# First stage of a four-layer graph network: roots by square root and reciprocal, work moved between GpSimd, VectorE and ScalarE

## The chip, the core and the metric

The kernel runs on one core of one Trainium2 chip. The core has a matrix engine (PE, with its weight loads shown apart as PEld), a vector engine (DVE), a scalar engine (ACT), GpSimd (POOL) and SyncE (SP), which here issues nearly all DMA transfers. The engines run side by side, each works its own instructions strictly in order, and they wait for each other by semaphores. SBUF is the working memory; PSUM takes the products of PE and can be read by DVE and ACT.

The metric is the device time of one execution in microseconds, the median of several runs.

## What is computed

The input is x, 128 graphs of 128 nodes with 128 features, and adj, an integer matrix of 128 x 128 for each graph, which the input generator fills with 0 and 1. Four layers of the form x = x + L(relu(layernorm(x))) follow each other. Cut to what matters here:

```python
def _layernorm(x, axis=-1, eps=1e-5):
    return (x - mean(x)) / sqrt(var(x) + eps)

# layer 0: relations r = 1..7
mask = (adj == r);  degree = clip(mask.sum(axis=2), 1e-6)
agg += ((mask / degree) @ h) @ rel_weights[r]
out = relu(layernorm(agg + h @ self_w.T + self_b) * gamma + beta)

# layer 1
D = abs(h[:, :, None, :] - h[:, None, :, :])     # every pair of nodes, 128 features
p = D @ W1.T + b1                                 # 64 features for every pair
p = leaky(normalised over all graphs and pairs) @ W2.T
A = softmax(where(adj > 0, p, -9e15));  y = A @ h ...

# layers 2 and 3: attention with adj > 0 as the mask
```

The dear part is D and its product: 128 graphs times 128 x 128 pairs. Since |a - b| is symmetric the kernel computes half of the pairs.

## The kernel before, in words

**Stages.** The first stage (to about 1528 us) does layer 0 and, tile by tile, the pair products of layer 1, which it stores to HBM (HP) together with their statistics. The second (to about 2330 us) reads them back, normalises and scores them and ends layer 1. The third does layers 2 and 3. The change touches the first stage alone.

**Tiles of pairs.** Graphs ("batches" in the code) are numbered b = 0 to 127, four of them (G) form a group, and there are 32 groups. Each batch has NT = 4 tiles of pair differences, tile i = 4 b + t. For one tile the steps are:

- ("d", i), `difference`, L311: one instruction of 128 x 2048 elements. If t is in ON_POOL = {1, 3} it is GpSimd's, else VectorE's. GpSimd reads both operands from SBUF (XE); VectorE reads one from SBUF and the other, x itself, from PSUM (XP). Tile t = 0 (BY_MAX) takes a maximum, the others a difference. The result goes to a tile d with two buffers for each of the two engines (tags d0, d1).
- ("abs", i), L352: ScalarE takes the absolute value in place, for t = 1 to 3.
- ("hp", i), L321 and L324: PE's products into PSUM, with two buffers.
- ("hs", i), L335: ScalarE copies the product to SBUF; ("st", i), L342 and L343: VectorE takes its statistics.

So 8 of the 16 tiles of a group are GpSimd's and 8 are VectorE's.

**The chain of a group.** `chain(g)` computes layer 0 for the four batches of a group and the input of the pair loop, some groups ahead of it. Its steps: load x and adj; `mask`, adj == 1 (GpSimd, L439), and its row sums (VectorE); `mv`, mean and variance of x (VectorE, L429 and L431); `rs`, the inverse root; `hn`, the normalised x with relu (ScalarE, four instructions, L452); transposes (PE) and their copies (ScalarE, L465); the products with the weights; `o`, the sum (VectorE); `mvo`, `rso`, `oc` and `on`, the second norm with gamma and beta from PSUM; `end`, the new x; `mvx` and `rsx` with the statistics for layer 1, and `h1`, its normalised relu (ScalarE, L493), from which the tiles start. In between GpSimd writes `m8` (L517), the mask adj > 0 as bytes, for the later stages.

A root, three in each chain, is four small GpSimd instructions on 128 x 4 elements: `rsqrt` adds eps (L224) and raises to the power of -0.5 (L225); `shift` multiplies with the mean (L280) and changes the sign (L281), which gives the bias of the following norm.

**What sets the order.** The steps are not run as they are written. Each `step(name, engine, cost, after, rank, work)` names its engine, an assumed cost in us, what it waits for and a rank; `_ordered` plays all steps of the stage through with these costs and a hop of 0.4 us between engines, always taking the step that can start first, and issues the instructions in the order so found. An engine then keeps that order whatever the real durations are. A difference waits, by its step, for the earlier difference i - 2 and for the product of tile i - 4, the earlier user of its buffer.

**The first microseconds.** The chains of the groups 0 and 1 run before a branch that asks whether adj holds anything above 1 (the path for that is not taken here), while all of adj is read for that question; the pair loop begins behind it at 48 us and runs freely from about 77 us.

The functions that the diff touches:

Of the kernel before, what the change touches and what calls it, by code (L numbers as in the profile page):

```python
# [14 lines left out]
OP = mybir.AluOpType  # L15
# [14 lines left out]
ROW = P + 2 * KH  # L30
ON_POOL = {1, 3}
BY_MAX = 0
AHEAD = 2
# [135 lines left out]
def tile_gnn_stack(ctx: ExitStack, tc: tile.TileContext, a: dict, out: bass.AP):  # L169
# [20 lines left out]
    mhalf = const.tile([P, 1], F32, name="mhalf")  # L190
    nc.gpsimd.memset(mhalf, -0.5)
    ones = const.tile([P, P], F32, name="ones")
    nc.vector.memset(ones, 1.0)
# [67 lines left out]
    with tc.tile_pool(name="c0", bufs=1) as c0, tc.tile_pool(name="p0", bufs=2) as p0, ExitStack() as ctx0:  # L261
# [14 lines left out]

        def shift(mv, rs):

            nb = small.tile([P, G], F32, name="lnnb")
            nc.gpsimd.tensor_tensor(nb, mv[:, :, 0], rs, OP.mult)  # L280
            nc.gpsimd.tensor_scalar(nb, nb, -1.0, None, op0=OP.mult)  # L281
            return nb


# [10 lines left out]
        def step(name, engine, cost, after, rank, work, takes=(), gives=()):  # L295
            steps.append((name, engine, cost, after, takes, gives, rank, work))

        XE, XW, diffs, linear, halves, stats = {}, {}, {}, {}, {}, {}

        def difference(i):  # L300

            b, t = divmod(i, NT)
            xe, k = XE[b // 2], b % 2
            on_pool = t in ON_POOL
            d = p0.tile([P, 2, KC, P], F32, tag=f"d{int(on_pool)}", name="d")
            x = xe[:, k, 0:P] if on_pool else XP[b // 2 % 2][:, k, :]
            ahead = xe[:, k, 1 + KC * t:]
            ahead = bass.AP(tensor=ahead.tensor, offset=ahead.offset,
                            ap=[list(ahead.ap[0]), [KH, 2], [1, KC], [1, P]])
            eng = nc.gpsimd if on_pool else nc.vector  # L310
            eng.tensor_tensor(d, ahead, x[:, None, None, :].to_broadcast([P, 2, KC, P]),  # L311
                              OP.max if t == BY_MAX else OP.subtract)
            diffs[i] = d.rearrange("p h k i -> p h (k i)")
# [40 lines left out]
        def pairs(i):  # L354

            b, t = divmod(i, NT)
            n, by_max = b // 2, t == BY_MAX
            engine, cost, rank = ("Pool", 4.22, i - 3) if t in ON_POOL else ("DVE", 2.2, i - 2)
            step(("d", i), engine, cost, [("again", n), ("d", i - 2), ("hp", i - 4)], rank, lambda: difference(i))
            if not by_max:  # L360
# [40 lines left out]
        def chain(g, agg=None, again=None):  # L401
# [22 lines left out]
            def moments(name):  # L424
# [5 lines left out]
                for k in range(G):  # L430
                    nc.vector.bn_aggr(mv[:, k, :], st[:, k, :])  # L431

            def roots(last=False):
                rs = t["rs"] = RS1[:, g] if last else small.tile([P, G], F32, name="lnrs")
                rsqrt(rs, t["mv"][:, :, 1])
                t["nb"] = shift(t["mv"], rs)

# [10 lines left out]
            def centred(dst, src, func=AF.Identity):  # L448
                if dst not in t:
                    tile0(dst)  # L450
                for k in range(G):
                    nc.scalar.activation(t[dst][:, k, :], t[src][:, k, :], func, bias=t["nb"][:, k:k + 1],  # L452
                                         scale=t["rs"][:, k:k + 1])

            def shared():
# [44 lines left out]
            else:  # L500
# [3 lines left out]
            step(("deg", g), "DVE", 0.6, own("mask"), s0 + 3.1, degree)  # L504
            step(("rs", g), "Pool", 1.95, own("mv"), s0 + 5, roots)
            step(("most", g), "Pool", 0.25, own("deg"), s0 + 5.1, at_least)
            step(("per", g), "DVE", 0.15, own("most"), s0 + 7, lambda: nc.vector.reciprocal(t["deg"], t["deg"]))
            step(("hn", g), "ACT", 1.55, own("rs"), s0 + 7, lambda: centred("hn", "x", AF.Relu))
            step(("share", g), "Pool", 1.05, own("per"), s0 + 9, shared)
            step(("pt", g), "PE", 0.55, own("hn"), s0 + 9, lambda: turned("hn"), takes=("sm",))  # L510
            step(("hT", g), "ACT", 0.5, own("pt"), s0 + 9.5, lambda: copied("hT", "pt"), gives=("sm",))
            step(("pm", g), "PE", 0.55, own("share", "hT"), s0 + 11, lambda: turned("mask"), takes=("sm",))
            step(("maskT", g), "ACT", 0.5, own("pm"), s0 + 12, lambda: copied("maskT", "pt"), gives=("sm",))
            step(("ph", g), "PE", 1.05, own("hT") + ["small"], s0 + 11.1, projected, takes=("sm",))
            step(("hw", g), "ACT", 0.5, own("ph"), s0 + 13, lambda: copied("hw", "ph"), gives=("sm",))
            step(("m8", g), "Pool", 1.5, own("load"), s0 + 11,
                 lambda: nc.gpsimd.tensor_scalar(M8[g], t["adj"], 0, None, op0=OP.is_gt))  # L517
            step(("po", g), "PE", 2.05, own("maskT", "hw"), s0 + 14, gathered, takes=("sm",))
            step(("o", g), "DVE", 0.6, own("po", "agg") + ["selfb"], s0 + 15, joined, gives=("sm",))
            step(("mvo", g), "DVE", 1.05, own("o"), s0 + 15.1, lambda: moments("o"))  # L520
            step(("rso", g), "Pool", 1.95, own("mvo", "hn"), s0 + 17, roots)
            step(("oc", g), "ACT", 1.55, own("rso"), s0 + 18, lambda: centred("o", "o"))
# [3 lines left out]
            step(("mvx", g), "DVE", 1.05, own("end"), s0 + 21.1, lambda: moments("MV1"))  # L526
            step(("rsx", g), "Pool", 1.95, own("mvx", "oc", "m8"), s0 + 23, lambda: roots(True))
            for half in range(2):
# [1073 lines left out]
```

## Time and profile before

| | |
|---|---|
| runs | 2803.65 us median of 3 (2803.29 to 2803.67) |
| profiled execution, span | 2798.6 us |
| around the span in that comparison | 5.05 us (median less span) |
| PE / DVE / ACT / POOL busy over the span | 2453.5 / 2474.2 / 2391.9 / 1720.2 us |
| first stage, steady part, one group | 45.6 us |
| first stage's pair loop ends | about 1528 us |

The page's busy times are means over stages with different limits; POOL's 61%, for instance, is near 95% in the first stage and small in the second. So the steady part of the first stage is read by itself below, group by group of sixteen tiles. In the rows, "x256" is the number of instructions, then come total busy us and mean ns of one, then the idle time of the engine just before them and what ended most of it.

### The profile page before, as it was taken

Reading aid. Unit: us, or ns where it says so; the run is one execution under the profiler, and the core shown is the slowest. Engines: PE = TensorE matmul, PEld = TensorE weight load, DVE = VectorE, ACT = ScalarE, POOL = GpSimd, SP = SyncE. Lnnn points to the kernel's source line nnn. Section 1 sums busy time; section 2 is a strip of 40 time slices with the busy share of each in tenths; the row PEclk is TensorE's granted clock in tenths of the full one; section 3 lists DMA queues with packets and bytes.
Section 4 is the critical chain, followed back from the end, with each engine's and each line's share of the span. In section 5 each row is a group of like instructions: output and inputs, shape, how many; then the busy total and the mean of one; then the engine's idle time right before and its main releaser. Section 6 shows DMA issues by size and latency. Waiting matters only on the chain.

```text
span 2798.6 us, 41745 instructions
## 1 busy us (share of the span) xinstructions
PE 2453.5 (88%) x14521; PEld 1178.8 (42%) x14521; DVE 2474.2 (88%) x4712; ACT 2391.9 (85%) x2837; POOL 1720.2 (61%) x1629
## 2 busy tenths in 40 slices
PE   3899999999999999999997798888888886999986
PEld 2333333333333333333332244444444444777775
DVE  4899999999999999999998588888888886899876
ACT  4799999999999999999997778877878765888975
POOL 6699999999999999999986001111000115555642
PEclk8899999999999999999999899999999998999998
DMA  7454555554555555554545999999999971121110
GB/s 285 169 207 202 204 207 212 213 211 200 207 202 208 207 218 207 207 211 200 207 203 217 418 410 412 411 413 411 411 412 413 413 266 46 46 67 59 58 31 25
DMA packets 179802, 652.40 MB, mean 233 GB/s; under 512 B 30963, under 2 KB 98678, under 8 KB 130422
## 3 DMA queue, kind: packets, MB, share of 16 engines
q1 hardware_dynamic: 179136, 649.39, 58.6%
q8 instruction: 120, 1.97, 0.3%
q14 instruction: 108, 0.88, 0.1%
q10 hardware_dynamic: 438, 0.17, 0.0%
HBM read 337.22 MB, written 312.28 MB: 232 GB/s over the span
## 4 chain that ended last, share of the span: by engine, by line
ACT 35%; PE 22%; DVE 21%; DMA 8%; issue 7%; POOL 5%; SPq 0%; ACTq 0%; DVEq 0%; POOLq 0%
ACT d L352 14%; ACT hs L335 10%; PE hp L321 5%; PE ps L853 5%; DVE z L896 4%; DVE d L311 3%; DMA rows<-sk 3%; POOL d L311 3%; DMA z<-hp 2%; DMA u<-rows 2%; PE hp L324 2%; PE pk L860 2%; ACT h L1206 2%; PE pv L1322 2%; ACT h L493 1%
## 5 line engine op out<-in xcount | busy, mean ns | idle before, releaser
L311 POOL TENSOR_TENSOR d<-xe 128x2048 f32<-128x2048 f32 x256 | 1074.1, 4201 | 59.0 <-PE hp L321 53.8
L321 PE MATMUL hp<-d,w1T 128*64 128x512 f32 x4096 | 997.1, 602 | 123.5 <-ACT hs L335 83.9
L352 ACT ACTIVATE d<-d 128x2048 f32<-128x2048 f32 x384 | 734.4, 1935 | 41.8 <-DVE d L311 22.9
L311 DVE TENSOR_TENSOR d<-xe,xp 128x2048 f32<-128x2048 f32 x256 | 579.4, 2263 | 4.7 <-PE hp L321 2.7
L321 PEld LDWEIGHTS hp<-d,w1T 128*64 128x64 f32 x4096 | 285.4, 137 | 642.1 <-issue 480.6
L335 ACT COPY hs<-hp 128x1024 f32<-128x1024 f32 x512 | 516.7, 1028 | 30.7 <-PE hp L324 24.0
L942 POOL TENSOR_TENSOR x<-x,bt 128x512 f32<-128x512 f32 x32 | 43.8, 1367 | 684.8 <-DMA x<-x 641.3
L342 DVE BATCH_NORM_STATS2 st<-hs 128x6 f32<-128x512 f32 x512 | 349.1, 682 | 43.5 <-ACT hs L335 43.1
L343 DVE BATCH_NORM_STATS2 st<-hs 128x6 f32<-128x512 f32 (+1 forms) x512 | 329.0, 643 | 0.0
L896 DVE SCALAR_TENSOR_TENSOR z<-z 128x2048 f32<-128x2048 f32 x128 | 295.1, 2306 | 21.7 <-ACT z L878 21.7
L878 ACT ACTIVATE z<-z,bias,scale 128x2048 f32<-128x2048 f32 x128 | 267.3, 2088 | 19.0 <-DMA z<-hp 19.0
L882 ACT ACTIVATE zr<-z,bias,scale 128x2048 f32<-128x2048 f32 x128 | 267.4, 2089 | 4.7 <-DMA z<-hp 3.8
L324 PE MATMUL hp<-both_t,xw 128*64 128x512 f32 x1024 | 268.1, 595 | 0.0
L853 PE MATMUL ps<-z,w2z 128*32 128x512 f32 x1024 | 143.8, 634 | 81.6 <-DVE z L896 81.6
L860 PEld LDWEIGHTS pk<-pick,su 128*128 128x128 f32 x1024 | 126.1, 194 | 134.4 <-DVE su L874 88.2
L860 PE MATMUL pk<-pick,su 128*128 128x16 f32 x1024 | 138.5, 267 | 17.6 <-DVE su L874 17.6
L1322 PE MATMUL pv<-wr,e 128*128 128x128 f32 x1024 | 140.5, 283 | 5.9 <-DVE e L1299 4.0
L853 PE MATMUL ps<-z,w2l 128*32 128x512 f32 x1024 | 143.1, 628 | 0.0
L324 PEld LDWEIGHTS hp<-both_t,xw 128*64 128x64 f32 x1024 | 80.7, 138 | 141.2 <-issue 141.2
L853 PE MATMUL ps<-zr,w2r 128*32 128x512 f32 x1024 | 139.9, 619 | 0.0
L1322 PEld LDWEIGHTS pv<-wr,e 128*128 128x128 f32 x1024 | 128.1, 196 | 13.3 <-DVE e L1299 4.1
L1299 DVE SCALAR_TENSOR_TENSOR e<-e,ps 128x512 f32<-128x512 f32 x160 | 106.9, 677 | 26.1 <-ACT ps L1296 25.4
(243 smaller groups left out, 3828.1 us busy)
## 6 DMA issues: line engine op xcount, KB each, us to landing
hp<-hs SPq DMA_DIRECT2D x128, 2048.0 KB, 6.3
z<-hp SPq DMA_DIRECT2D x256, 1024.0 KB, 14.3
x<-x SPq DMA_DIRECT2D x118, 256.0 KB, 11.6
u<-rows SPq DMA_DIRECT2D x32, 384.0 KB, 11.4
x<-in_x_dram SPq DMA_DIRECT2D x32, 256.0 KB, 3.0
adj<-in_adj_dram SPq DMA_DIRECT2D x32, 256.0 KB, 3.3
part<-in_adj_dram SPq DMA_DIRECT2D x16, 512.0 KB, 7.8
out_dram<-x SPq DMA_DIRECT2D x32, 256.0 KB, 2.4
```

The lines of the kernel that those rows point to most:

```text
L311: eng.tensor_tensor(d, ahead, x[:, None, None, :].to_broadcast([P, 2, KC, P]), OP.max if t == BY_MAX else OP.subtract)
L321: nc.tensor.matmul(hp[64 * hh:64 * hh + 64, c:c + 512], w1T2 if by_max else w1T, d[:, hh, c:c + 512], start=True, stop=not by_max, skip_gr ...
L324: nc.tensor.matmul(hp[64 * hh:64 * hh + 64, c:c + 512], XW[i // NT // 2][:, i // NT % 2, :], both_t.rearrange("p h k i -> p h (k i)")[:, h ...
L335: nc.scalar.copy(halves[b][:, t, :], linear.pop(i))
L342: nc.vector.bn_stats(st[:, 2 * t, :], hs[:, 0:512])
L343: nc.vector.bn_stats(st[:, 2 * t + 1, :], hs[:, 512:1024 - P * last])
L352: nc.scalar.activation(diffs[i], diffs[i], AF.Abs)
L853: nc.tensor.matmul(ps[32 * c:32 * c + 32, :], w[:, w0:w0 + 32], v[:, 512 * c:512 * c + 512], start=j0 == 0, stop=w is w2r, skip_group_chec ...
L860: nc.tensor.matmul(pk[:, kk, 0:16], su[:, kk, :], pick.rearrange("p h j -> p (h j)"), start=True, stop=True)
L882: nc.scalar.activation(zr, z1, AF.Relu, bias=bias1, scale=scale1[:, 0:1])
L896: nc.vector.scalar_tensor_tensor(z0, z0, 0.01, z0, op0=OP.mult, op1=OP.max)
L1322: nc.tensor.matmul(t[pv][:, k % 2, hd, :], t[e][:, hd, :], flat[:, at:at + P], start=True, stop=True)
```

## The change

- A root is now a ScalarE square root of variance + eps (step `sd`, `sdo`, `sdx`), followed on VectorE by a reciprocal and one scalar_tensor_tensor that makes the bias, minus mean times root. eps is a new constant tile. GpSimd has no part in it any more.
- `hn`, the first of the three norms, moves from ScalarE to GpSimd (four tensor_scalar, multiply and add with a value per row); its relu moves into ScalarE's copy of the transpose, which is there already.
- Nine of the sixteen tiles of a group are GpSimd's: beside t = 1 and 3 also tile 2 of the group's fourth batch. The waits for the earlier difference and the earlier user of the buffer are looked up for the engine concerned.
- `m8` is made by a minimum with 1 and a maximum with 0 in place of a comparison.
- The assumed costs of these steps are changed accordingly, so the order of the whole stage is found anew.

```diff
+EXTRA_ON_POOL = (3, 2)
...
+    eps = const.tile([P, 1], F32, name="eps")
+    nc.gpsimd.memset(eps, EPS)
...
-        def shift(mv, rs):
-            nb = small.tile([P, G], F32, name="lnnb")
-            nc.gpsimd.tensor_tensor(nb, mv[:, :, 0], rs, OP.mult)
-            nc.gpsimd.tensor_scalar(nb, nb, -1.0, None, op0=OP.mult)
-            return nb
...
+        def by_pool(i):
+            b, t = divmod(i, NT)
+            return t in ON_POOL or (b % G, t) == EXTRA_ON_POOL
+
+        def earlier(i, n):
+            return [j for j in range(i) if by_pool(j) == by_pool(i)][-n] if i >= 3 * n else -1
...
-            engine, cost, rank = ("Pool", 4.22, i - 3) if t in ON_POOL else ("DVE", 2.2, i - 2)
-            step(("d", i), engine, cost, [("again", n), ("d", i - 2), ("hp", i - 4)], rank, lambda: difference(i))
+            engine, cost, rank = ("Pool", 4.22, i - 3) if by_pool(i) else ("DVE", 2.2, i - 2)
+            step(("d", i), engine, cost, [("again", n), ("d", earlier(i, 1)), ("hp", earlier(i, 2))], rank,
+                 lambda: difference(i))
...
+            def deviation():
+                t["sd"] = small.tile([P, G], F32, name="lnsd")
+                nc.scalar.activation(t["sd"], t["mv"][:, :, 1], AF.Sqrt, bias=eps)
+
             def roots(last=False):
                 rs = t["rs"] = RS1[:, g] if last else small.tile([P, G], F32, name="lnrs")
-                rsqrt(rs, t["mv"][:, :, 1])
-                t["nb"] = shift(t["mv"], rs)
+                nc.vector.reciprocal(rs, t["sd"])
+                t["nb"] = small.tile([P, G], F32, name="lnnb")
+                nc.vector.scalar_tensor_tensor(t["nb"], t["mv"][:, :, 0], -1.0, rs, op0=OP.mult, op1=OP.mult)
...
+            def normed():
+                for k in range(G):
+                    nc.gpsimd.tensor_scalar((t["hn"] if k else tile0("hn"))[:, k, :], t["x"][:, k, :],
+                                            t["rs"][:, k:k + 1], t["nb"][:, k:k + 1], op0=OP.mult, op1=OP.add)
...
-            step(("rs", g), "Pool", 1.95, own("mv"), s0 + 5, roots)
+            step(("sd", g), "ACT", 0.25, own("mv"), s0 + 4, deviation)
+            step(("rs", g), "DVE", 0.3, own("sd"), s0 + 5, roots)
...
-            step(("hn", g), "ACT", 1.55, own("rs"), s0 + 7, lambda: centred("hn", "x", AF.Relu))
+            step(("hn", g), "Pool", 1.4, own("rs"), s0 + 7, normed)
...
-            step(("hT", g), "ACT", 0.5, own("pt"), s0 + 9.5, lambda: copied("hT", "pt"), gives=("sm",))
+            step(("hT", g), "ACT", 0.5, own("pt"), s0 + 9.5, lambda: copied("hT", "pt", AF.Relu), gives=("sm",))
...
-            step(("m8", g), "Pool", 1.5, own("load"), s0 + 11,
-                 lambda: nc.gpsimd.tensor_scalar(M8[g], t["adj"], 0, None, op0=OP.is_gt))
+            step(("m8", g), "Pool", 0.8, own("load"), s0 + 11,
+                 lambda: nc.gpsimd.tensor_scalar(M8[g], t["adj"], 1, 0, op0=OP.min, op1=OP.max))
...
-            step(("rso", g), "Pool", 1.95, own("mvo", "hn"), s0 + 17, roots)
+            step(("sdo", g), "ACT", 0.25, own("mvo"), s0 + 16, deviation)
+            step(("rso", g), "DVE", 0.3, own("sdo", "hn"), s0 + 17, roots)
...
-            step(("rsx", g), "Pool", 1.95, own("mvx", "oc", "m8"), s0 + 23, lambda: roots(True))
+            step(("sdx", g), "ACT", 0.25, own("mvx"), s0 + 22, deviation)
+            step(("rsx", g), "DVE", 0.3, own("sdx", "oc", "m8"), s0 + 23, lambda: roots(True))
```

More of the change, by code (lines that the diff above doesn't have):

```diff
@@ L303, in difference @@
             xe, k = XE[b // 2], b % 2
-            on_pool = t in ON_POOL
+            on_pool = by_pool(i)
             d = p0.tile([P, 2, KC, P], F32, tag=f"d{int(on_pool)}", name="d")
```

## The prediction

> **What bounds the kernel now.** I read the stretches of the span first, then the groups of instructions, the waits and the order in time. The evacuations of tile 0 of the groups 4 to 28 start 45.6 us apart, so nine groups fill the stretch from 718.4 to 1129.2 us (columns: length, then busy time and count of PE, PEld, DVE, ACT, POOL, then clock, DMA share, GB/s):
>
> ```profile
> 718.40:1129.20 410.80, 382.44 (x1838) 148.47 (x1836) 398.13 (x685) 390.81 (x424) 389.15 (x235) 1.00 0.52 208
> ```
>
> Divided by nine, a group's 45.64 us hold 44.24 us of DVE, 43.42 of ACT, 43.24 of POOL and 42.49 of PE: four engines within 4%, with DVE fullest. DMA, at 0.52, has room. The groups, from the page (idle time and its releaser after the second bar):
>
> ```profile
> L311 POOL TENSOR_TENSOR d<-xe 128x2048 f32<-128x2048 f32 x256 | 1074.1, 4201 | 59.0 <-PE hp L321 53.8
> L352 ACT ACTIVATE d<-d 128x2048 f32<-128x2048 f32 x384 | 734.4, 1935 | 41.8 <-DVE d L311 22.9
> L311 DVE TENSOR_TENSOR d<-xe,xp 128x2048 f32<-128x2048 f32 x256 | 579.4, 2263 | 4.7 <-PE hp L321 2.7
> ```
>
> A difference tile costs POOL 4.20 us and DVE 2.26. The waits of DVE from 310 to 1403 us (24 periods: total, times, longest) are almost one row, 1.3 us a group:
>
> ```profile
> DVE st L342 <- ACT hs L335: 30.5, 46, 1.2
> ```
>
> So no engine waits long; the time is the load of the fullest one plus about 1.4 us. The change's other rows, grouped by form inside those nine groups, and the reciprocal from 70 to 1850 us:
>
> ```profile
> L225 POOL TENSOR_TENSOR lnrs<-lnrs,mhalf 128x4 f32<-128x4 f32 x19 | 19.7, 1037 | 1.6
> L452 ACT ACTIVATE hn<-x,lnnb,lnrs 128x128 f32<-128x128 f32 x36 | 15.0, 521 | 0.0
> L517 POOL TENSOR_SCALAR m<-adj 128x512 uint8<-128x512 int32 x9 | 13.5, 1502 | 0.7
> L507 DVE RECIPROCAL deg<-deg 128x4 f32<-128x4 f32 x30 | 4.8, 160 | 0.0
> ```
>
> What decides is found outside the pair loop. Lines in order of time (start, length), from the next stage:
>
> ```profile
> 1662.51 1.27 POOL L942 TENSOR_TENSOR x<-x,bt 128x512 f32<-128x512 f32 x1 [21.12 <-DMA x<-x]
> 1662.62 1.71 DVE L965 TENSOR_TENSOR e<-e,sums 128x512 f32<-128x512 f32 x1
> ```
>
> The same DVE instruction took 0.68 us at 1899.90, where it started 0.06 us before POOL's. Here it started 0.11 us after and took 1.03 us more: it held DVE until 0.13 us before POOL's end, then did its 0.67. Its spread over 32, and that of the byte mask:
>
> ```profile
> L965 DVE TENSOR_TENSOR e<-e,sums x32: 662/1053/1778, 1617.6 to 2327.4; 128x512 f32<-128x512 f32 x32
> L517 POOL TENSOR_SCALAR m<-adj x32: 1492/1502/3520, 8.7 to 1413.6; 128x512 uint8<-128x512 int32 x32
> ```
>
> The 3520 ns is the reverse case, behind DVE's two-input L602. In the pair loop no DVE instruction reads two operands from SBUF: L311, L479, L483, L484 and L487 each have one in PSUM, and their times are flat.
>
> **What the Trainium skill says.** "SBUF — State Buffer", Who interferes with whom: a VectorE instruction with two SBUF inputs and a GpSimd instruction that reads SBUF exclude each other, and the later one waits. The trace agrees (1.71 against 0.68 us). "ScalarE: Activation LUTs", Table sets: absolute value, copy, identity and relu are in every set, sqrt and exp in different ones. The trace shows one table load, 1.28 us, in the whole program; it cannot show sqrt.
>
> **The change part by part**, per group of 45.64 us.
>
> *Roots.* Removed from POOL: three times add (0.23), power (1.04), product (0.20) and negation (0.24), 1.71 each: −5.13. Added to ACT: three sqrt of 128x4. Nearest row: L392, 128x128, 0.30; with a pointer for the bias the skill's page gives 0.28, less 0.09 of overlap. Between 0.2 and 0.3; I take 0.2: +0.6. Added to DVE: three reciprocals (0.16, L507) and three scalar_tensor_tensor; L575, the same operation on 128x1 beside an idle POOL, took 0.16: +0.96.
>
> *Lock.* The new scalar_tensor_tensor reads mean and root, both from SBUF. If POOL is then in a difference tile, DVE waits for the rest. With nine tiles in some 48 us POOL is in one 9 × 4.2 / 48 = 0.79 of the time; the mean rest is (4.20 − 0.13) / 2 = 2.03; so 1.6 us each, 4.8 a group. Bounds: 0 (all three beside other work, or four elements slip through) and 3 × 4.07 = 12.2. Since the loop repeats exactly, the three waits will be nearly the same in every group, so luck is not averaged out. I take the mean. Queued behind the held instruction on DVE are the next difference and the statistics; ACT's absolute value waits for the first, PE for that.
>
> *Norm to POOL.* ACT loses 4 × 0.52, which overlap to 1.55. POOL gains four 128x128 tensor_scalar: from 4 × 0.25 (a fixed part like the 0.23 of L224) to 4 × 0.40 (a quarter of L439's 1.5): I take +1.3. Relu moves into a copy that exists: nothing.
>
> *Ninth tile.* DVE −2.26, POOL +4.20. In the fourth batch of a group the tiles 1, 2 and 3 are now all POOL's, followed two tiles later by the next: four tiles, 16.8 us, within five tile periods (14.3 us), with two buffers.
>
> *Byte mask.* POOL's 1.50 becomes something between 0.62 (L940's shortest: multiply and add over as many elements) and 1.50: I take 0.8, −0.7. Nothing waits for it soon.
>
> *Sums.* POOL 43.24 − 5.13 + 4.20 + 1.3 − 0.7 = 42.9. ACT 43.42 − 1.55 + 0.6 = 42.5. PE 42.5. DVE 44.24 − 2.26 + 0.96 = 42.94, and with the lock 47.8. DVE is then the bound; a late DVE finds its evacuations ready, so of its 1.4 us of waiting I keep 0.3: 48.1 us a group, +2.5. The chains of the groups 2 to 31 run in some 29 such periods: +72 us.
>
> *Ends.* Before the pair loop ACT waits for roots (2.71 and 1.85 us behind POOL's lnnb at 34.0 and 41.1 us); a root then takes about 0.8 us in place of 2.05, twice on that path: −2.5. The last groups have no chain and POOL's ninth tile is in the open: about +1.3. A second table load, for the first exp: at most +1.3, in a stage that waits for DMA (share 0.97). Another memset on POOL, 0.1 us while the first load is in flight: nothing. No DMA is added or moved past another by the edit; the planner reorders the stage for new costs, which I put at ±0.4 us a group. Together about 0.
>
> The profiled execution had 2798.6 us; +72 gives 2870.6. The median of the runs, 2803.65, stands 5.05 above: 2875.
>
> **Rivals.**
>
> *Relief (ends faster).* The lock does not bite: the three small instructions fall beside gaps, or their few elements get through. Then the fullest engine carries 42.9 and, with the same 1.4 us, a group takes 44.3: −1.3 × 29 = −38, so 2766. For it: ACT carries most of the chain that ended last here (ACT's lines L352 and L335 55% of it from 764 to 855 us) and gets lighter. It decides when the three waits stay under 1.3 us together. Against: POOL would have to be outside its tiles almost every time.
>
> *POOL's bunch or the hand-over.* Without much lock, three tiles in a row with two buffers leave PE waiting for POOL, or DVE waits in order for ACT's sqrt, which stands behind 1.9 us absolute values. One to two us a group eat the relief: 45.6 to 46.3, 2800 to 2825. For it: POOL already waits for PE's release (53.8 us of 59.0). Against: chunks of 12.6 us against two buffered tiles are short, and the planner places the hand-over.
>
> *Table switches.* If sqrt forces a load each way, six loads of 1.28 us a group put ACT at 50.2 and the group at about 52: +190, 2990 or more. The skill's page speaks against it.
>
> **How the numbers follow.** A measurement tells about 0.2% (5.6 us) from no change. Lock 0.63, its own range 2810 to 2945 (waits of 2.7 to 7.3 us a group; three waits of spread 1.3 us each); relief 0.20; bunch or hand-over 0.13; table switches 0.04. Slower: 0.60 of the lock, 0.09 of the bunch, 0.04 of the switches, 0.73. Same: 0.02 and 0.03, 0.05. Faster: 0.20, 0.01 of lucky lock, 0.01 of the bunch, 0.22. The range of 2765 to 2950 leaves out half of the relief (0.10), the switches (0.04) and the upper end of the lock (0.05).
>
> **What would show it.** Right: the new lnnb on DVE has a mean of 1.5 us or more against its shortest 0.16, a spread up to 4 us, the groups lie about 48 us apart, and POOL's idle time grows to 5 us a group. Wrong: lnnb flat near 0.16 us, or long but in time that DVE would have waited. Table loads more than two, or PE's waits for POOL's d, would point to the other rivals. L517 near 0.8 and the norm near 1.3 us for four check the sums.

## The result, and the profile after

| | before | after |
|---|---|---|
| median of the runs | 2803.66 us | 2986.39 us |
| ratio, 95% interval | | 1.0655, [1.064, 1.067] |
| span of the profiled execution | 2798.6 us | 2985.5 us |
| first to last evacuation of the pair loop | 56.0 to 1528 us | 58.1 to 1720 us |
| what follows it | 1271 us | 1266 us |

The change makes the kernel 183 us slower, far outside the range that was forecast. All of it lies in the first stage. The 29 periods between the starts of the groups 2 and 31 took 1502 us in place of 1324, which is 178 of the 187 us by which the spans differ; the rest is 9 us before and 5 us in the last group, less 5 us behind the loop.

The steady part does not repeat from group to group any more, but every three groups (47.3, 59.8 and 50.1 us, 52.4 on average). Nine groups, in the same columns as the stretch shown of before:

```profile
471.70:943.20 471.50, 396.57 (x1837) 148.94 (x1837) 452.24 (x730) 388.35 (x414) 389.29 (x172) 0.95 0.45 181
```

A group's 52.39 us hold 50.25 of DVE, 43.15 of ACT, 43.25 of POOL and 44.06 of PE (at a granted clock of 0.95, against 1.00 before). DVE has grown by 6.0 us, PE by 1.6 at the lower clock, and ACT and POOL stayed. The loss does not need the lower clock: e4 below had 1.00 in its pair loop and is 151 us slower than the kernel before. The groups of the page:

```profile
L315 POOL TENSOR_TENSOR d<-xe 128x2048 f32<-128x2048 f32 x288 | 1207.8, 4198 | 240.3 <-PE hp L325 186.5
L356 ACT ACTIVATE d<-d 128x2048 f32<-128x2048 f32 x384 | 730.5, 1911 | 16.6 <-POOL d L315 10.3
L315 DVE TENSOR_TENSOR d<-xe,xp 128x2048 f32<-128x2048 f32 x224 | 506.9, 2263 | 4.6 <-PE hp L325 2.4
```

The tiles cost what they did, 4.20 and 2.26 us, and 32 of them have moved; POOL's idle time before its tiles has gone from 59 to 240 us, most of it behind PE. Where DVE's time went is seen in the rows of the same nine groups for the instruction that makes the bias:

```profile
L446 DVE SCALAR_TENSOR_TENSOR lnnb<-lnmv,lnrs 128x4 f32<-128x4 f32 x18 | 48.3, 2685 | 0.6
L446 DVE SCALAR_TENSOR_TENSOR lnnb<-MV,RS 128x4 f32<-128x4 f32 x9 | 22.0, 2445 | 0.3
```

Four elements a row take 2.6 us. In the groups on their tile (shortest, median, longest in ns) the same instruction is seen from its free time up to nearly a whole tile of POOL:

```profile
L446 DVE SCALAR_TENSOR_TENSOR lnnb<-lnmv,lnrs x64: 161/2917/3936, 10.7 to 1610.3; 128x4 f32<-128x4 f32 x64
```

And in order of time, one of them beside the tile that holds it:

```profile
967.72 4.19 POOL L315 TENSOR_TENSOR d<-xe 128x2048 f32<-128x2048 f32 x1 [1.01 <-PE hp L325]
...
968.11 3.82 DVE L446 SCALAR_TENSOR_TENSOR lnnb<-MV,RS 128x4 f32<-128x4 f32 x1
```

It starts 0.39 us into the tile and ends 0.02 us behind it. Per group the three instructions take (48.3 + 22.0) / 9 = 7.81 us, of which 0.48 is their own work: 7.3 us of holding. Without it DVE would carry 42.92 us, and the prediction's sum says 42.94. The waits of DVE in the nine groups:

```profile
DVE st L346 <- ACT hs L339: 14.5, 7, 3.1
DVE o L498 <- ACT o L462: 4.9, 3, 1.6
```

That is 2.2 us a group: DVE is late and still waits. About half of it, 9.4 of the 20 us, stands before the statistics of one tile (counted in order, sixteen to a group): the third of the three that POOL takes in a row. The other new rows, from 719 to 1129 us:

```profile
L467 POOL TENSOR_SCALAR hn<-x,lnrs,lnnb 128x128 f32<-128x128 f32 x32 | 14.0, 453 | 0.8
...
L533 POOL TENSOR_SCALAR m<-adj 128x512 uint8<-128x512 int32 x7 | 4.3, 612 | 0.0
```

The norm is dearer than assumed (about 1.75 us for four, against 1.3), the byte mask cheaper (0.61 against 0.8). The table was loaded twice in the whole program, 1.28 us each, once for the first square root at 5.0 us and once before the first exponential of the second stage.

### The profile page after: what moved, and what is told of

Its sections match the earlier page's. It is cut to its first block, busy times and chain, and to the rows that moved or that the text cites. A ratio compares the mean times of both kernels' runs of the same rounds, so it can differ in the third digit from the quotient of the medians.

```text
span 2985.5 us, 41519 instructions
## 1 busy us (share of the span) xinstructions
PE 2498.8 (84%) x14521; PEld 1185.5 (40%) x14521; DVE 2631.0 (88%) x4872; ACT 2380.2 (80%) x2806; POOL 1724.6 (58%) x1406
## 4 chain that ended last, share of the span: by engine, by line
DVE 46%; PE 22%; ACT 16%; DMA 6%; issue 5%; POOL 2%; SPq 0%; DVEq 0%; POOLq 0%; ACTq 0%
DVE d L315 10%; ACT d L356 6%; DVE st L346 6%; PE hp L325 5%; DVE st L347 5%; PE ps L871 5%; DVE lnnb L446 5%; DVE z L914 4%; ACT hs L339 4%; DMA z<-hp 3%; PE pk L878 2%; ACT h L1224 2%; PE hp L328 1%; DVE lnst L434 1%; DMA rows<-sk 1%
## 5 line engine op out<-in xcount | busy, mean ns | idle before, releaser
L315 POOL TENSOR_TENSOR d<-xe 128x2048 f32<-128x2048 f32 x288 | 1207.8, 4198 | 240.3 <-PE hp L325 186.5
L325 PE MATMUL hp<-d,w1T 128*64 128x512 f32 x4096 | 1031.0, 628 | 260.8 <-ACT d L356 141.5
L339 ACT COPY hs<-hp 128x1024 f32<-128x1024 f32 x512 | 509.3, 1007 | 92.9 <-PE hp L325 62.7
L315 DVE TENSOR_TENSOR d<-xe,xp 128x2048 f32<-128x2048 f32 x224 | 506.9, 2263 | 4.6 <-PE hp L325 2.4
L446 DVE SCALAR_TENSOR_TENSOR lnnb<-lnmv,lnrs 128x4 f32<-128x4 f32 x64 | 148.0, 2312 | 2.2
```

The source lines that it names most:

```text
L325: nc.tensor.matmul(hp[64 * hh:64 * hh + 64, c:c + 512], w1T2 if by_max else w1T, d[:, hh, c:c + 512], start=True, stop=not by_max, skip_gr ...
L339: nc.scalar.copy(halves[b][:, t, :], linear.pop(i))
L446: nc.vector.scalar_tensor_tensor(t["nb"], t["mv"][:, :, 0], -1.0, rs, op0=OP.mult, op1=OP.mult)
```

## The experiments

Two theories of the result stood against each other. *Lock*: the loss is DVE held by POOL's tiles. *Hand-over and bunch*: the loss, or much of it, comes from ScalarE's square root between two VectorE steps, from the three tiles in a row on GpSimd, or from the new order. All medians are of runs beside runs of the kernel before on the same chip (2802 to 2804 us). The last column is the mean over the groups 8 to 16; for e5 and e16, which repeat in other steps, over the groups 4 to 27.

| run | what it is | median us | ratio to before | us a group |
|---|---|---|---|---|
| e1_columns | the change, bias by one-input instructions | 2876 | 1.0265 [1.0248, 1.0282] | 47.8 |
| e2_before_two | before, three two-input instructions more | 2953 | 1.0536 [1.0516, 1.0555] | 51.2 |
| e3_before_one | before, three one-input instructions more | 2814 | 1.0038 [1.0024, 1.0052] | 45.6 |
| e4_roots_alone | before, with the change's roots alone | 2955 | 1.0543 [1.052, 1.0565] | 51.4 |
| e5_roots_bias_pool | the same, bias by GpSimd | 2802 | 0.9995 [0.9986, 1.0004] | 46.1 |
| e6_columns_three | e1 with three buffers | 2778 | 0.9903 [0.9886, 0.9919] | 45.2 |
| e7_columns_norm_act | e1 with the norm on ScalarE | 2843 | 1.0142 [1.0125, 1.0159] | 47.0 |
| e8_mean_three | e6, no bias for the first root, other costs | 2800 | 0.9985 [0.9978, 0.9992] | 45.9 |
| e9_lock_three | the change with three buffers | 3033 | 1.0829 [1.081, 1.0847] | 53.7 |
| e10_mean_three_order | e6, no bias for the first root | 2777 | 0.9913 [0.9896, 0.9929] | 45.2 |
| e11_before_three | before with three buffers | 2769 | 0.9886 [0.987, 0.9903] | 44.6 |
| e12_three_same_order | e1 with three buffers, order of e1 | 2871 | 1.0251 [1.0234, 1.0268] | 48.2 |
| e13_columns_prices | e1, planner told the true costs | 2860 | 1.0205 [1.0188, 1.0222] | 47.9 |
| e14_lock_prices | the change, planner told the true costs | 2969 | 1.0591 [1.0569, 1.0613] | 51.2 |
| e15_bias_pool_nine | e5 with nine tiles and three buffers | 2787 | 0.9942 [0.9925, 0.9959] | 45.5 |
| e16_bias_pool_nine_two | e5 with nine tiles and two buffers | 2896 | 1.0336 [1.0319, 1.0353] | 48.5 |

### Taking the second input away: e1

```diff
-                nc.vector.scalar_tensor_tensor(t["nb"], t["mv"][:, :, 0], -1.0, rs, op0=OP.mult, op1=OP.mult)
+                for k in range(G):
+                    nc.vector.tensor_scalar(t["nb"][:, k:k + 1], t["mv"][:, k, 0:1], rs[:, k:k + 1], -1.0,
+                                            op0=OP.mult, op1=OP.mult)
```

> The changed kernel, where only the bias of a norm is made otherwise: in place of one scalar_tensor_tensor of 128x4 with two SBUF tensors, four tensor_scalar of one column each (mean, times the root as a value per row, times -1), which read one tensor. Order and assumed costs stay. Lock theory (the two-input instruction is held until GpSimd's running difference tile ends, and that is nearly the whole loss): VectorE's 50.1 us a group lose 7.2 us of holding and gain about 0.8 us of small instructions, 43.7; a group takes 45 us in place of 52.4, and the run 2765 to 2795 us. Hand-over theory (ScalarE's square root between two VectorE steps, the three GpSimd tiles in a row and the new order cost most of it, the holding fell into time that would have been waited anyway): 2900 us or more.

2876 us, between the two ranges: 110 of the 183 us are gone, and 72 stay. The mean and the root now reach VectorE as one tensor and one value per row, and POOL does not hold that, as the groups on the bias tile show:

```profile
L447 DVE TENSOR_SCALAR lnnb<-lnmv,lnrs x256: 199/204/217, 10.4 to 1504.1; 128x1 f32<-128x1 f32 x128
```

Flat over 256. So taking the lock away gave 110 us here, although VectorE now has about 1.3 us a group more of small instructions (0.58 us for four columns in place of 0.16), and neither theory alone gives the result. Nine groups of this run:

```profile
459.40:889.70 430.30, 384.05 (x1837) 147.80 (x1837) 399.49 (x811) 386.90 (x415) 387.77 (x172) 0.99 0.50 198
```

47.81 us a group hold 44.39 of DVE, 42.99 of ACT and 43.09 of POOL: the fullest engine is hardly fuller than before (44.24), and yet 3.4 us are waited in place of 1.4.

### The lock by itself: e2 and e3

In `moments`, behind the aggregates, of the kernel before, e2 adds the second and e3 the third line of this:

```diff
+                spare = small.tile([P, G], F32, name="spare")
+                nc.vector.scalar_tensor_tensor(spare, mv[:, :, 0], -1.0, mv[:, :, 1], op0=OP.mult, op1=OP.mult)
+                nc.vector.reciprocal(spare, mv[:, :, 1])
```

> The kernel before with one instruction more in each of the three moments of a chain: a scalar_tensor_tensor of 128x4 on VectorE that reads two SBUF tensors (mean and variance) into a tile that nobody reads. Nothing else changes, no engine waits for it. Lock theory: GpSimd is in a tile 8 x 4.2 / 49 = 0.69 of the time, so about 1.4 us each if the moments fall anywhere, 4.2 us a group, 2900 us, and up to 2985 if they fall early in a tile as in the changed kernel; the instruction's mean well over 1 us. Hand-over theory: three instructions of 0.16 us, 2804 to 2820 us.

> The same as the run beside it, but the instruction added reads one tensor: a reciprocal of 128x4 of the variance into a tile that nobody reads. Both theories: 0.16 us each or less, 2804 to 2820 us. If this run is as slow as the one with two inputs, it is not the second input that costs, and the lock theory falls.

2953 and 2814 us, 139 us apart. Nobody waits for either instruction. They differ in the second tensor and in the operation, but the shortest product takes 161 ns and the reciprocal 177 to 180, so it is the second tensor that costs. In the stretch from 489 to 1420 us (18 groups) of e2:

```profile
L433 DVE SCALAR_TENSOR_TENSOR spare<-MV 128x4 f32<-128x4 f32 x18 | 51.5, 2861 | 0.6
...
L433 DVE SCALAR_TENSOR_TENSOR spare<-lnmv 128x4 f32<-128x4 f32 x36 | 29.5, 820 | 1.2
```

(51.5 + 29.5) / 18 − 0.48 = 4.0 us of holding a group, near the 4.2 of random places; the period grew by 5.6 (45.6 to 51.2). The instructions themselves cost the period nothing: e3's stays at 45.6, and 7 of the 9 us by which its span is longer lie behind the pair loop, which the edit doesn't touch. So a microsecond of holding cost about 1.4 of time here. That is no constant: between e1 and the change 7.3 us of holding come with 4.6 of time. The theory of a late VectorE that finds everything ready is wrong: e2's VectorE carries 48.7 of 51.2 us and waits 2.5.

### The roots alone: e4, and without the lock: e5

e4 puts the change's square root, reciprocal and two-input instruction into the kernel before and nothing else; e5 is e4 with

```diff
-                nc.vector.scalar_tensor_tensor(t["nb"], t["mv"][:, :, 0], -1.0, rs, op0=OP.mult, op1=OP.mult)
+            step(("rsb", g), "Pool", 0.5, own("rs"), s0 + 5.05, biased)     # product and sign on GpSimd, as before
```

and the same for the other two roots.

> The kernel before with the roots alone as in the change (square root on ScalarE, reciprocal and two-input scalar_tensor_tensor on VectorE); eight of sixteen tiles on GpSimd, the first norm on ScalarE and the byte mask by comparison as before. Lock theory: VectorE 44.2 + 1.0 + 4 to 7 us of holding, 49.5 to 53 us a group with what is waited, 2900 to 3000 us: all of the loss or more without the ninth tile. Rival (the loss comes from nine tiles in bunches and from the norm on GpSimd): the hand-over alone costs at most 1.5 us a group, 2790 to 2850 us.

> The kernel before (eight tiles on GpSimd, norm on ScalarE, mask by comparison) with the roots by ScalarE's square root and VectorE's reciprocal, but the bias still made by GpSimd's two small instructions, so that VectorE has no two-input instruction. It holds the hand-over VectorE - ScalarE - VectorE - GpSimd without the lock and without the ninth tile. Hand-over theory (what is left of the loss without the lock, 72 us, comes from these waits): 2850 us or more. Bunch theory (it comes from GpSimd's three tiles in a row with two buffers): loads of VectorE 44.7, ScalarE 44.0, GpSimd 39.6 us, a group 45.6 to 46.2 us, 2800 to 2822.

e4 2955, e5 2802 us. The roots as the change makes them cost 151 us by themselves; with the bias where it was they cost nothing. So the hand-over VectorE - ScalarE - VectorE by itself is not what the 72 us are: that part of the rival theory falls. In the stretch from 489 to 1420 us e4's granted clock was 1.00, and its groups take 51.4 us all the same.

### Where the other 72 us are: e6, e7, e12

For e6 the difference tiles of GpSimd get a third buffer, and their step waits for the third tile back; six in place of eight buffers for reading adj make room:

```diff
-            d = p0.tile([P, 2, KC, P], F32, tag=f"d{int(on_pool)}", name="d")
+            d = p0.tile([P, 2, KC, P], F32, tag=f"d{int(on_pool)}", name="d", bufs=2 + on_pool)
-            step(("d", i), engine, cost, [("again", n), ("d", earlier(i, 1)), ("hp", earlier(i, 2))], rank,
+            step(("d", i), engine, cost, [("again", n), ("d", earlier(i, 1)),
+                 ("hp", earlier(i, 3 if by_pool(i) else 2))], rank,
```

> The changed kernel with the bias by one-column instructions (no lock), and three buffers in place of two for GpSimd's difference tiles; to make room the reading of adj at the start has six buffers in place of eight. Bunch theory: GpSimd no longer waits for PE to free its tiles and PE no longer for the absolute value, the group falls from 47.8 to about 45.8 us, 2805 to 2825. Hand-over theory: the buffers change nothing, 2860 to 2885.

e7 is e1 with `hn` as before:

```diff
-            step(("hn", g), "Pool", 1.4, own("rs"), s0 + 7, normed)
+            step(("hn", g), "ACT", 1.55, own("rs"), s0 + 7, lambda: centred("hn", "x", AF.Relu))
```

> The changed kernel with the bias by one-column instructions, and the first norm back on ScalarE with its relu; nine tiles on GpSimd as in the change. Loads: VectorE 44.4, ScalarE 44.0, GpSimd 41.4. If the norm on GpSimd, in the way of its tiles, makes what is left of the loss: 2800 to 2825. Bunch theory: still slow, 2850 to 2890, since the tiles in a row stay.

e6 is at 2778, below both ranges and 1% faster than the kernel before; e7 at 2843, between the two ranges: moving the norm back gives 33 of the 72 us, by the load or by the order, which this run doesn't tell apart. e6 looked like a wait for a buffer. But e6 changes two things, the buffer and what the planner is told, and with it the order. e12 keeps e6's third buffer and the planner's old rule:

```diff
-                 ("hp", earlier(i, 3 if by_pool(i) else 2))], rank,
+            step(("d", i), engine, cost, [("again", n), ("d", earlier(i, 1)), ("hp", earlier(i, 2))], rank,
```

> The changed kernel with one-column instructions and three buffers for GpSimd's tiles, where the planner is still told that the buffer of the tile before last must be free, so that the pair loop's order stays that of the run with one-column instructions and two buffers. If the wait for a buffer costs (bunch theory), 2780 to 2810; if it was the new order that the planner found with the third buffer, it stays at 2860 to 2880.

2871 us. The third buffer alone gives 5 us of the 98 between e1 and e6, and the intervals of the two ratios overlap; the order that the planner finds when it may count on it gives 93. e12 and e6 run the same instructions with the same buffers, and from group 8 to 25 e12's trace has e1's order on POOL, ACT and DVE. What POOL waits for in e12 from 489 to 1420 us (in total, times, longest):

```profile
POOL xe L402 <- ACT xe L389: 43.9, 19, 4.2
POOL mask L451 <- DMA adj<-in_adj_dram: 35.0, 18, 5.2
...
POOL d L315 <- PE hp L325: 2.3, 7, 0.4
```

In e1 the same stretch has this and next to nothing else:

```profile
POOL d L315 <- PE hp L325: 86.4, 70, 3.1
```

So the third buffer did free POOL of that wait, and it was turned into another at once: POOL is early, and stands in order before the feature copy and the mask. PE's wait for absolute values stays as long, in e12

```profile
PE hp L325 <- ACT d L356: 71.4, 40, 4.2
```

against 71.5 in e1. In e6 it is

```profile
PE hp L325 <- ACT d L356: 13.5, 21, 0.6
```

One of PE's long waits, in e12, in order of time on POOL:

```profile
914.77 4.20 POOL L315 TENSOR_TENSOR d<-xe 128x2048 f32<-128x2048 f32 x1 [0.39 <-PE hp L325]
923.12 0.29 POOL L402 COPY xe<-xe 128x128 f32<-128x128 f32 x1 [4.15 <-ACT xe L389]
924.86 1.50 POOL L451 TENSOR_SCALAR mask<-adj 128x512 f32<-128x512 int32 x1 [1.45 <-DMA adj<-in_adj_dram]
926.33 8.32 POOL L315 TENSOR_TENSOR d<-xe 128x2048 f32<-128x2048 f32 x2
```

and on PE:

```profile
934.14 4.20 PE L325 MATMUL hp<-d,w1T 128*64 128x512 f32 x12 [4.22 <-ACT d L356]
```

The copy for the next two batches and the mask stand between the second and the third of the three tiles in a row. The third can't start before 926.33, 7.4 us after the second ended; it is ready at 930.5, ACT has a norm and a copy of PSUM ahead of it in its own order and takes it at 932.17, and PE has stood since 929.92. In e1 the same place has the same wait of 4.22 us, to 931.87: there the third tile starts at 924.92, behind the same copy and mask. In e6 POOL has:

```profile
866.45 4.20 POOL L315 TENSOR_TENSOR d<-xe 128x2048 f32<-128x2048 f32 x1
871.50 4.19 POOL L315 TENSOR_TENSOR d<-xe 128x2048 f32<-128x2048 f32 x1 [0.85 <-PE hp L325]
875.64 0.28 POOL L402 COPY xe<-xe 128x128 f32<-128x128 f32 x1
875.91 1.50 POOL L451 TENSOR_SCALAR mask<-adj 128x512 f32<-128x512 int32 x1
877.38 0.61 POOL L535 TENSOR_SCALAR m<-adj 128x512 uint8<-128x512 int32 x1
879.09 12.53 POOL L315 TENSOR_TENSOR d<-xe 128x2048 f32<-128x2048 f32 x3 [1.11 <-PE hp L325]
```

Counted from the first tile, nine to a group, the tiles at 866.45 and 871.50 are the second and third of the bunch. Copy and masks stand behind the third, and the three in one row after them are the next group's first.

Whether PE's wait costs time is read from VectorE, the fullest engine. After the wait of 4.22 us in e1 it loses only 0.85 us. Its longest waits, 4.11 us, come in other groups, but again before the statistics of the third tile. One of them, on POOL and on DVE:

```profile
875.45 0.29 POOL L402 COPY xe<-xe 128x128 f32<-128x128 f32 x1
875.83 0.23 POOL L458 TENSOR_SCALAR deg<-deg 128x4 f32<-128x4 f32 x1
876.16 1.74 POOL L469 TENSOR_SCALAR hn<-x,lnrs,lnnb 128x128 f32<-128x128 f32 x4
877.87 8.35 POOL L315 TENSOR_TENSOR d<-xe 128x2048 f32<-128x2048 f32 x2
...
889.56 0.69 DVE L346 BATCH_NORM_STATS2 st<-hs 128x6 f32<-128x512 f32 x1 [4.11 <-ACT hs L339]
```

Here copy, degree and norm hold the third tile back to 877.87. Its product is done at 886.25, and ScalarE takes it at 888.49, behind a copy and another absolute value, so ScalarE's order has its part too. In the nine groups of e1 VectorE waits 15.7 of some 31 us before the statistics of this one tile.

So the bunch theory holds in another form than I put it: what costs is not a wait for a buffer at run time but the order that the planner finds under the rule of two buffers, in which POOL's third tile stands behind other work and its product reaches VectorE late. That an order costs 93 us is shown by e12 and e6; that it is this part of the order is read from the traces, and no run moved these instructions alone.

### Is it the ninth tile, or the planner's costs? e13, e14, e15, e16

In e13 and e14 the planner is told what the traces show: 0.72 us (e13) or, with the lock, 2.8 (e14) for a root on VectorE in place of 0.3; 1.72 for the norm; 0.6 for the byte mask. The first of the five lines that e13 edits:

```diff
-            step(("rs", g), "DVE", 0.3, own("sd"), s0 + 5, roots)
+            step(("rs", g), "DVE", 0.72, own("sd"), s0 + 5, roots)
```

> The changed kernel with one-column instructions (no lock, two buffers), where the planner is told the durations that the traces show: 0.72 us for a root on VectorE in place of 0.3, 1.72 for the norm on GpSimd in place of 1.4, 0.6 for the byte mask in place of 0.8. If the order was bad because of wrong assumed costs, it comes down to 2775 to 2810; if two buffers and nine tiles leave the planner no good order, it stays within 15 us of 2876.

> The changed kernel, two-input instruction and two buffers as in the change, where the planner is told 2.8 us for a root on VectorE (0.2 and the mean holding of 2.6), 1.72 for the norm and 0.6 for the byte mask. The holding stays: VectorE 42.9 + 4.8 to 7.2 us a group, so 2865 at best. If an order made for the holding helps, 2870 to 2940; if the place of the held instruction in GpSimd's tiles decides, anything between 2865 and 3030, and the mean of the held instruction goes with it.

e13 at 2860, a microsecond past the range for no help: true costs give 16 of the 72 us. e14 at 2969: the order has changed so far that 36 of 54 two-input instructions now fall outside POOL's tiles,

```profile
L446 DVE SCALAR_TENSOR_TENSOR lnnb<-MV,RS 128x4 f32<-128x4 f32 x18 | 16.0, 887 | 0.6
...
L446 DVE SCALAR_TENSOR_TENSOR lnnb<-lnmv,lnrs 128x4 f32<-128x4 f32 x36 | 6.0, 166 | 1.2
```

and the holding is down to 0.7 us a group; but a group still takes 51.2 us. VectorE now waits some 6 us of it for ScalarE's evacuations (111 us in the stretch), about the time that was set aside for the holding. The change is not saved by telling the planner of the lock.

e15 is e5 with nine tiles, three buffers for them, and the mask by minimum and maximum; e16 is e15 with two buffers and their rule. Cut to two of the edited places (the last line is e16's in place of the one above it):

```diff
-            on_pool = t in ON_POOL
+            on_pool = by_pool(i)                                             # nine of sixteen
-            d = p0.tile([P, 2, KC, P], F32, tag=f"d{int(on_pool)}", name="d", bufs=2 + on_pool)
+            d = p0.tile([P, 2, KC, P], F32, tag=f"d{int(on_pool)}", name="d")
```

> A version meant to be faster than all: roots by square root and reciprocal, the bias by GpSimd's two small instructions, nine tiles on GpSimd with three buffers, the norm on ScalarE, the mask by minimum and maximum. Loads a group: VectorE 42.5, ScalarE 44.0, GpSimd 42.8, PE 42.5 us. If the load decides, 44.2 to 44.8 us, 2745 to 2770; if the order does, above 2770.

> The run e15 with two buffers in place of three for GpSimd's tiles, and the planner told so (and eight buffers for the reading of adj again); same instructions, no two-input instruction, norm on ScalarE. Beside the run with eight tiles and the same roots (e5, 2802) it holds the ninth tile, its cheaper byte mask, and nothing else of weight. If nine tiles with two buffers leave the planner no good order, 2825 to 2860, and e15's gain is the third buffer's; if the rest of the loss was in the norm on GpSimd or the small instructions on VectorE, 2780 to 2800.

2787 and 2896 us, the second above both of its ranges. Without the lock, with the norm on ScalarE and no small instructions on VectorE but three reciprocals, going from eight tiles (e5, 2802) to nine costs 94 us with two buffers and gains 15 with three. So the rest of the loss goes with nine tiles planned for two buffers, but its size does not follow from that alone: e7 too has nine tiles, two buffers and the norm on ScalarE, and stands only 40 us above the kernel before. (e16 and e5 differ in the cheaper byte mask and in the cost assumed for the reciprocal too, 0.1 against 0.3.) Since e12 shows that one more buffer alone hardly helps, the planned order is the likely cause here too; e16's order was not run with three buffers.

### Lock and order together: e9

e9 is the change as it is, with e6's two lines for three buffers.

> The changed kernel with its two-input scalar_tensor_tensor, but three buffers for GpSimd's tiles (and six for the reading of adj): the fourth corner of the square lock / no lock, two / three buffers. If the two causes add, it lies 98 us under the changed kernel, at 2888; by the loads, VectorE carries 42.9 and 4.8 (random places) to 7.2 us (places as in the changed kernel) of holding, 48.1 to 50.5 us a group, 2865 to 2940. If the holding only hurt because the tiles were short of buffers, it comes down to about 2780.

3033 us, worse than the change, and outside all its forecasts. The costs don't add: in e6's order the lock costs 255 us, in the change's order 110. From 489 to 1420 us:

```profile
L446 DVE SCALAR_TENSOR_TENSOR lnnb<-lnmv,lnrs 128x4 f32<-128x4 f32 x36 | 138.8, 3855 | 1.2
...
L446 DVE SCALAR_TENSOR_TENSOR lnnb<-MV,RS 128x4 f32<-128x4 f32 x17 | 36.0, 2119 | 0.6
```

Two of the three instructions of a group reach POOL always 0.2 to 0.5 us after a tile has begun, the worst place there is, and wait nearly all of it, in every group.

### Versions meant to be faster: e8, e10, e11

e8 and e10 let GpSimd's norm subtract the mean and multiply with the root, so that the first root needs no bias:

```diff
-                                            t["rs"][:, k:k + 1], t["nb"][:, k:k + 1], op0=OP.mult, op1=OP.add)
+                                            t["mv"][:, k, 0:1], t["rs"][:, k:k + 1], op0=OP.subtract, op1=OP.mult)
```

They differ in the assumed costs alone (e8: 0.1, 0.5, 0.5; e10: 0.3 as in the change).

> A version meant to be faster: as the run with three buffers, and GpSimd's norm subtracts the mean and multiplies with the root, so that the first root needs no bias and VectorE loses four one-column instructions a group; the assumed costs are 0.1 for that root and 0.5 for the other two. Lock and bunch theory together: VectorE 43.7, GpSimd 43.2, ScalarE 42.5, a group of 45.0 to 45.4, 2780 to 2800. Hand-over theory: 2850 or more.

> A version meant to be faster: the run with three buffers and one-column instructions, where GpSimd's norm subtracts the mean and multiplies with the root (no bias for the first root, four instructions less on VectorE a group); the assumed costs stay those of the change, so the order stays close to that run's. VectorE falls from 44.2 to 43.6 us a group, GpSimd stays near 43: 44.7 to 45.2 us a group, 2762 to 2780 us. If the order decides more than the load, it may end above 2780.

2800 and 2777: the same work, 22 us apart by the planner's costs, and e10 no better than e6 although VectorE has less to do. e11 is the kernel before with a third buffer for GpSimd's tiles:

```diff
-            step(("d", i), engine, cost, [("again", n), ("d", i - 2), ("hp", i - 4)], rank, lambda: difference(i))
+            step(("d", i), engine, cost, [("again", n), ("d", i - 2), ("hp", i - (6 if t in ON_POOL else 4))], rank, ...
```

> The kernel before with three buffers for GpSimd's tiles (and six for the reading of adj), nothing else. Its waits of GpSimd for PE are 1.0 us a group and VectorE carries 44.2 of 45.6: at most 1.4 us a group to gain, 2770 to 2806. If it lands at 2778, the third buffer alone makes the gain of the run with three buffers, and the moved work none.

2769 us, ratio 0.9886: the fastest of all, with none of the moved work. Nine groups:

```profile
433.20:834.40 401.20, 377.18 (x1836) 144.96 (x1834) 396.00 (x682) 391.33 (x425) 388.94 (x235) 1.00 0.53 211
```

44.58 us a group, 44.0 of them VectorE's work: within 0.6 us of the load of the fullest engine. Whether the buffer or the order that came with it did this was not taken apart here.

## Why the prediction was wrong

**Direction and mechanism held.** Slower was given 0.73, and the first cause named is there: the two-input instruction is held to the end of POOL's tile. The mean of 2.6 us of that instruction (lnnb) and its spread up to 3.9 us are as the last paragraph described them; POOL's idle time grew further, to 7.5 us a group in place of 5, and the groups lie 52.4 us apart in place of 48. The loads of VectorE, ScalarE and GpSimd came out within 0.7 us of the sums: 42.92 without the holding (42.94), 43.15 (42.5) and 43.25 (42.9). PE was busy for 44.06 in place of 42.5, at a clock of 0.95. Relief and table switches did not occur. Relief was possible, as one rival had it: e6 shows 26 us of it, without the lock and with another order.

**What failed is the size: +72 forecast, +187 measured in the span.** A group took 52.4 us in place of 48.1. Of the 4.3 us, 2.5 are holding and 1.8 are waiting. These are the steps:

- *"Of its 1.4 us of waiting I keep 0.3"*, with *"the planner reorders the stage for new costs, which I put at ±0.4 us a group"*. This is the step that failed most. VectorE waited 2.1 us a group (52.39 less 50.25). The holding missed by more, but stayed inside the prediction's own bounds: with the measured 7.3 us of holding and only 0.3 of waiting its sum gives the 2945 that it names as the lock's upper end. The waiting is what lies beyond. The order makes 3.4 us of waiting without any lock (e1), and 94 us go with the ninth tile under the rule of two buffers (e16 against e5). In e2, where nothing but the holding was added, VectorE waits 2.5, so a late VectorE does not find everything ready either.
- *"I take the mean."* 4.8 us of holding a group were assumed, 7.3 measured. The prediction said itself that luck is not averaged out, and then took the average. Nor were the waits the same in every group, since the order repeats every three. In the change's order 48 of 54 of the instructions fall into a tile, on average 1.3 us after its start and not in its middle; in e2's order the holding is 4.0 us, in e9's 9.4 (two instructions at 138.8 / 36, and 36.0 over 17 for the third, less 0.48).
- The bunch was counted as a rival *without much lock*, at 0.13; it came on top of the lock. And its form was wrong: PE does wait for POOL's third tile, by way of ScalarE, but a third buffer that leaves the order alone gives 5 us (e12).

One agreement is partly luck. Between relief (2766) and its forecast (2875) the prediction has 109 us for the lock, and between e1 and the change 110 were measured. But there was half as much holding again, and e1 has small instructions that the prediction's relief has not. What was missed lies under the lock: without it 38 us were to be gained, and e1 loses 72.

The ends, put at about 0 together, were small but of the other sign: the pair loop started 2.1 us later and not 2.5 earlier, and the last group took 41.9 us in place of 37.3.

What stays open: how the 72 us that e1 keeps divide. True costs give 16 of them back (e13), and the norm on ScalarE 33 (e7, in an order of its own). How much the late third tile makes was seen in the traces and not tested alone; and why e9's order meets POOL's tiles at their start while the change's spreads over them was not tested.

## What to carry to other kernels

When an operation moves to VectorE beside a busy GpSimd, count its SBUF tensors: in this kernel a second one cost the rest of the difference tile that GpSimd was in, though the operation had four elements a row, and it was cheaper to give that operand as a value per row, or to leave the work where it was. Where every engine is over 90% full and the order is fixed ahead, a sum of loads gives the floor and not the time: a rule of the plan (how many buffers it may assume) moved this kernel by 93 us with the same instructions and buffers. And an experiment that changes a buffer and the plan together needs its twin that changes the buffer alone.

## What the runs showed of the hardware

- A scalar_tensor_tensor of 128 x 4 with two SBUF tensors took 0.16 us free and up to 3.94 us beside GpSimd's tile (the change); a tensor_scalar of 128 x 1 with a value per row took 0.20 us whatever GpSimd did (199 to 217 ns over 256 in e1), and a reciprocal of 128 x 4 0.14 to 0.18.
- The hold is not the same beside every GpSimd instruction. Beside the comparison of 128 x 512 integers (1.50 us) the scalar_tensor_tensor took 0.16 to 0.36 us with 0.6 to 1.2 us of the comparison still to run (one case in the change, three in e2), so the rule quoted in the prediction is wider than what was measured. And it can outlast one tile: in e9 one started at 143.80, 0.25 us before the end of a tile, and ended at 153.92, 0.02 us behind the second of two further tiles. GpSimd had run these, with a product before and a mask between them, without a pause.
- GpSimd's mask of 128 x 512 integers to bytes took 1.50 us by comparison and 0.61 by minimum and maximum.
- The square root of 128 x 4 with a bias tile took 0.30 us on ScalarE, no more than the other small activations, with one table load for all of the stage.
